# Three outer products of a kernel's first pass in the form of seven inner products instead of eight

## The chip, the cores and the metric

The kernel runs on one core of one Trainium2 chip. The metric is the device time of one execution in microseconds (us), as the median of several runs. One more execution is taken with the hardware profiler; its page and its trace are what the durations below come from. In them PE is TensorE's matmuls, PEld its weight loads, DVE is VectorE, ACT is ScalarE, POOL is GpSimd and SP is SyncE, whose queue issues nearly all DMAs.

## The reference, cut to what matters

The reference is two layers of a block, in float32, on 8 x 256 tokens of width 512. The change concerns the attention of the first layer alone:

```python
qkv = jax.nn.silu(hidden_states @ qkv_w.T)          # 2048 x 512 by 512 x 12288
...                                                 # 32 heads of 128: linear attention with decay
normed = norm_w * xf.astype(attn.dtype)             # after a root mean square over all heads
gate = jax.nn.sigmoid(hidden_states @ gate_w.T)     # 2048 x 512 by 512 x 4096
return gate * normed @ out_w.T
```

The product of tokens with the weights of q, k, v and gate is the largest piece of work in the whole computation. A mixture of 16 experts, a second attention and a low-rank layer follow or run beside it; the change doesn't touch them.

## The kernel before, in words

**Tiling.** The 2048 tokens are cut into four chunks of 512 (i = 0 to 3), the 32 heads into eight groups of four (g = 0 to 7). One unit (i, g) is the product of a chunk with the 2048 columns of weights of one group (q, k, v and gate of four heads). Four passes, one a chunk, run over the eight groups. The list `plan` (line 1071) holds all 4 x 8 x 7 outer products in their order.

**Two levels of seven.** A unit's product is a two by two block product. It is made of seven products of sums of blocks instead of eight products of blocks (Strassen's scheme in Winograd's form). These are the seven outer products, in the order `ORDER`: p1, p2, p6, p5, p3, p7, p4. Each is a two by two block product again. One inner product (`product`, line 661) is four matmuls, which work on weights of 128x512 and tokens of 128x128. In the second to fourth pass an outer product is made of seven inner products, which need weights and tokens summed a second time (inner sums). In the first pass it is made of eight, on plain blocks (`plain`, line 981).

**What the first pass makes for the others.** The weights come from the input `w_att` in four blocks of 128x512, 1 MB in all. Three outer products, p1, p2 and p4 (`RAW`, line 29), take blocks as they are. p6, p5 and p7 load one or two more operands (`block`, tag `xw`, two buffers, 1 MB each) and p3 takes p6's (`previous`), and VectorE sums them (`outer_sum`, four steps, each of one or two instructions). Then GpSimd makes four inner sums (`inner_sum`, line 634), the last of which is followed by a store of the sums to `ws`, from where the later passes load them. Plain products read the weights' four blocks, raw or with VectorE's sums, but no inner sum. Outer and inner sums are steps, kept in a list: `plain` runs those that its own outer product has left, and then, after each inner product but the first, one of the following outer product's (`following.step()`). The tokens of the first pass are in seven tiles (`first_x`), each holding four blocks; the other passes load their seven blocks from `xc`.

**Rings.** Weights are in a ring of three tiles (`big`, line 123). `prepare(n + 2)` (line 1164) makes the outer product two places on: it takes the tile of outer product n - 1 and issues its loads. The tile is free when TensorE has done n - 1's last product and the store to `ws` has landed. PSUM gives products four banks: two named `ps_a`, one `ps_b`, one `ps_e`.

**The form of seven.** In the later passes the methods `p1`, `p7`, `p6`, `p4`, `p2`, `p5`, `p3` of `Outer` (lines 1037 to 1066) issue one inner product each. Some banks are used twice: p6 adds into p1's bank, so p1's value is first copied out by ScalarE (`copied`, line 994, tag `cp`, five buffers), and likewise p7's and p6's. `p3` of an outer product runs only after `p1` and `p7` of the next. `result` (line 999) takes one of the four quarters out of its bank. Given a copy c, it adds bank and c on VectorE, and what is then still to be added is added by GpSimd (lines 1016 and 1028, by way of a buffer named r with tag `sum`, three buffers). Without a copy it adds or copies straight out of the bank, on VectorE or ScalarE.

**What runs between.** After each inner product `slot` (line 679) runs pieces that are due: the attention of a quarter (scores, attend), the output projection, and in the first pass the rows of tokens (`row`, also tag `sum`) that GpSimd scatters into `xd` for the experts.

**Order.** ScalarE's and GpSimd's instructions run in the order in which the program issues them (line 599). The orders of TensorE, VectorE and SyncE are the framework's planner's.

**The opening** (lines 140 to 523) normalizes, routes, and makes the token sums of each chunk (`token_sums`, line 369): for chunk 0 into `first_x`, for the others, with their inner sums, into `xc`.

Of the kernel before, what the change touches and what calls it, by code (L numbers as in the profile page):

```python
# [28 lines left out]
RAW = dict(p1=0, p2=1, p4=3)  # L29
# [37 lines left out]
def block_kernel(  # L67
# [25 lines left out]
    nc = tc.nc  # L93
# [73 lines left out]
    for i in range(1, NCH):  # L167
# [36 lines left out]
        out=before, in_=before, pattern=[[1, E], [-1, E]], compare_op=ALU.is_gt,  # L204
# [11 lines left out]
        out=dist[:, 0:S], in_=dist[:, 0:S], pattern=[[1, S]], compare_op=ALU.is_ge,  # L216
# [137 lines left out]
    def sub(o, a, b, eng=None):  # L354
        tt(o, a, b, ALU.subtract, eng)
# [8 lines left out]

    HC = NC // 2

    first_x, first_w = {}, []

    def token_sums(i):

        def blocks(v):
            return v.rearrange("p (c t) n -> p c t n", c=2)

        def tile_():
            return work.tile([P, 4, P], FP, tag="xsum", name="xsum", bufs=3)

        quarter = {  # L380
            (j, l): xT[i][:, bass.ts(j, HC), bass.ts(l, S)].rearrange("p c (t n) -> p c t n", t=2)
            for j, l in QUARTERS
        }
        with_ = None
        if i == 0:
            for p in ORDER:
                first_x[p] = toks.tile([P, 7, P], FP, tag="X", name="xt")
        for p, at in (
            ("p1", (0, 0)), ("p2", (1, 0)), ("p3", (1, 1)),
            ("p5", (0, 1)), ("p6", (1, 1)), ("p4", (1, 0)), ("p7", (1, 1)),  # L390
        ):
            y = quarter[at]
            if p in ("p5", "p6", "p4", "p7"):
                o = {"p5": quarter[0, 0], "p7": quarter[0, 1]}.get(p, with_)
                with_ = blocks(tile_() if i else first_x[p][:, 0:4])
                sub(with_, y, o, nc.gpsimd)
                y = with_
            if i == 0:
                if y is not with_:
                    nc.sync.dma_start(out=blocks(first_x[p][:, 0:4]), in_=y)  # L400
                continue
            nc.sync.dma_start(out=blocks(xc[i][:, ORDER.index(p), 0:4]), in_=y)
            t = tile_()
            sub(t[:, 0], y[:, 0, 1], y[:, 0, 0], nc.gpsimd)
            sub(t[:, 3], y[:, 1, 1], y[:, 0, 1], nc.gpsimd)
            sub(t[:, 1], y[:, 1, 1], t[:, 0], nc.gpsimd)
            sub(t[:, 2], y[:, 1, 0], t[:, 1], nc.gpsimd)
            nc.sync.dma_start(out=xc[i][:, ORDER.index(p), 4:8], in_=t)
# [14 lines left out]
    for i in range(NCH):  # L423
# [7 lines left out]
        if i == 0:  # L431
            for p in ORDER[0:2]:
                w = big("w")
# [21 lines left out]
        out=earlier, in_=earlier, pattern=[[1, P]], compare_op=ALU.is_gt,  # L455
# [25 lines left out]
    at = NTT * E  # L481
# [117 lines left out]
    with tc.tile_pool(name="attn", bufs=1) as attn, tc.manual_schedule(engines={mybir.EngineType.Activation, mybir.EngineType.Pool}):  # L599
# [5 lines left out]
        def weights(i, g, p, steps):  # L605

            loaded = len(first_w) > 0
            w = first_w.pop(0) if loaded else big("w")  # L610
            y = w[:, 0:4]
            v = nc.vector
            pool = nc.gpsimd

            def block(n):
                st = staged("st")[:, 0 : 16 * P].rearrange("p (b n) -> p b n", b=4)
                nc.sync.dma_start(out=st, in_=w_att[g, n])
                return st

            if i == 0:  # L620
                if not loaded:
                    nc.sync.dma_start(out=y, in_=w_att[g, dict(RAW, p6=2, p5=2, p3=1, p7=0)[p]])
                outer = dict(p6=[(add, 3), (sub, 0)], p5=[(add, 3)], p7=[(sub, 2)]).get(p, ())
                outer = [(f, block(n)) for f, n in outer]
                if p == "p3":
                    outer = [(sub, previous["s2"])]
                if p == "p6":
                    previous["s2"] = y

                def outer_sum(n):  # L630
                    for f, other in outer:
                        f(y[:, n], y[:, n], other[:, n], v)

                def inner_sum(f, o, a_, b_):
                    f(w[:, o], w[:, a_], w[:, b_], pool)
                    if o == 7:
                        nc.sync.dma_start(out=ws[g][p], in_=w[:, 4 if p in RAW else 1 : 8])

                if outer:
                    steps += [partial(outer_sum, n) for n in (1, 2, 0, 3)]  # L640
                steps += [
                    partial(inner_sum, *at) for at in ((add, 4, 0, 3), (sub, 5, 4, 1), (sub, 6, 2, 5), (sub, 7, 1, 0))
                ]
                return {at: w[:, n] for n, at in enumerate(((1, 0), (0, 0), (0, 1), (1, 1)))}
            if p in RAW:
                nc.sync.dma_start(out=y, in_=w_att[g, RAW[p]])
                nc.sync.dma_start(out=w[:, 4:8], in_=ws[g][p])
            else:
                nc.sync.dma_start(out=w[:, 1:8], in_=ws[g][p])
            return dict(zip(("p1", "p2", "p4", "p5", "p6", "p3", "p7"), (w[:, n] for n in range(1, 8))))  # L650

        def tokens(i, p):
            if i == 0:
                return {q: first_x[p][:, n] for n, q in enumerate(QUARTERS)}
            t = toks.tile([P, 7, P], FP, tag="X", name="xt")
            x_ = xc[i][:, ORDER.index(p)]
            nc.sync.dma_start(out=t[:, 0], in_=x_[:, 0])
            nc.sync.dma_start(out=t[:, 1:7], in_=x_[:, 2:8])
            return dict(zip(("p1", "p2", "p3", "p5", "p6", "p4", "p7"), (t[:, n] for n in range(7))))

        def product(bank, w, xx, first):

            for ty in range(4):
                w_ = w[:, bass.ts(ty, P)]
                a, b = (w_, xx) if ty < 3 else (xx, w_)
                mm(  # L666
                    bank[:, bass.ts(ty, P)], a, b, start=(first and ty == 0), stop=True,
                    skip_group_check=True,
                )


        pieces = []
# [6 lines left out]
        def slot():  # L679

            now[0] += 1
            n = 0
            while pieces and pieces[0][0] <= now[0] and n < (2 if len(pieces) > 12 else 1):
                f = pieces.pop(0)[2]
                f()
                n += getattr(f, "func", f).__name__ not in ("silu", "gate", "row", "scatter", "load_sum", "sums1", "sums2", "sums3", "sums4", "settle0", "settle1", "out_sum")
# [273 lines left out]
        class Outer:  # L960


            def __init__(self, unit, p):
                self.u, self.p = unit, p
                self.steps = []
                self.w = weights(unit.i, unit.g, p, self.steps)
                if unit.g == 0:
                    Outer.x_[p] = tokens(unit.i, p)
                self.x = Outer.x_[p]

            x_ = {}

            def go(self, bank, p, first=False):
                product(bank, self.w[p], self.x[p], first)
                slot()

            def step(self):
                if self.steps:
# [185 lines left out]
        def prepare(n):  # L1164
            if n < len(plan):
                outers.append(make(n))
            elif n == len(plan):
# [4 lines left out]
                for t in range(TPC):  # L1172
                    later(2 + 2 * t, lambda t=t: turn_rows(yT0, settled[0], t, ps_sc()))

        wsm = yT0 = None
        outers = [make(0), make(1)]
        for n, (i, g, p) in enumerate(plan):
            if i == 0 and p == "p5":
                for _ in range(4):
                    outers[n + 1].step()  # L1180
            cur = outers[n]
            u = cur.u
            k = ORDER.index(p)
            if k == 0:
                u.load_decay()
                if i * NG + g >= FROM:
                    for e in range(3 if i * NG + g < FROM + EARLY else 2):
                        if todo:
                            later((20 if g == 0 and i > 1 else 1) + 16 * e, partial(expert, todo.pop(0)))
                if i == 0:  # L1190
                    for e in range(2):
                        later(1 + 24 * e, partial(row, 2 * g + e))
                if i == NCH - 1 and g in (NG - 4, NG - 3):
                    low_sums(g - NG + 4)
                if (i, g) == (NCH - 1, NG - 2):
                    wrapped_up()
            if k == 2:
                u.load_decay()
            u.load_out(k)
            if i == 0:  # L1200
                prepare(n + 2)
                cur.plain(outers[n + 1])
                continue
            cur.p1()
            cur.p7()
            if plan[n - 1][0] > 0:
                outers[n - 1].p3()
            prepare(n + 2)
            cur.p6()
            cur.p4()  # L1210
            cur.p2()
            cur.p5()
# [409 lines left out]
```

## Time and profile before

| what | time |
|---|---|
| median of 3 runs | 2856.99 us (2852.0 to 2861.1) |
| the profiled execution | 2856.16 us |
| its span in the profile | 2854.4 us |
| opening (0 to 164) | 164 us |
| first pass (164 to 763) | 599 us |
| second, third and fourth pass | 607, 588 and about 574 us to the last product |
| the rest: second layer | from about 2532 us |

The page gives the busy time of each engine in the whole span, in a second part in 40 equal slices, each digit a share in tenths. Busy TensorE matmuls are pipelined, so the duration of one isn't what the next one waits: that is read from the starts. In a timeline's row stand start, length, engine, line, instruction, tile written and read, shapes, count, and in brackets how long the engine had been idle and what released it. In the table by stage, each row is a stretch with the busy time of each engine, the granted clock of TensorE, and DMA's share and rate. Line 97 is the helper `tt`, by which every add and subtract is recorded, so its rows are told apart by tiles.

### The profile page before, as it was taken

Reading aid. Unit: us, or ns where it says so; the run is one execution under the profiler, and the core shown is the slowest. Engines: PE = TensorE matmul, PEld = TensorE weight load, DVE = VectorE, ACT = ScalarE, POOL = GpSimd, SP = SyncE. Lnnn points to the kernel's source line nnn. Section 1 sums busy time; section 2 is a strip of 40 time slices with the busy share of each in tenths; the row PEclk is TensorE's granted clock in tenths of the full one; section 3 lists DMA queues with packets and bytes.
Section 4 is the critical chain, followed back from the end, with each engine's and each line's share of the span. In section 5 each row is a group of like instructions: output and inputs, shape, how many; then the busy total and the mean of one; then the engine's idle time right before and its main releaser. Section 6 shows DMA issues by size and latency. Waiting matters only on the chain. (4 is left out here: it accounts for less than half of the span.)

```text
span 2854.4 us, 49572 instructions
## 1 busy us (share of the span) xinstructions
PE 2796.7 (98%) x19864; PEld 2566.1 (90%) x19864; DVE 1569.7 (55%) x2615; ACT 948.2 (33%) x1683; POOL 1465.7 (51%) x1213
## 2 busy tenths in 40 slices
PE   8989999999999999999999999999999999999999
PEld 4469999999999999999999999999999999987877
DVE  6555666666654445444545555555555555556663
ACT  3312222212244333333443333443444333432221
POOL 4545666665546555555645454545544566552210
PEclk9999999999999999999999999999999999999999
DMA  7888998899986777778877777777777788652211
GB/s 255 301 309 337 357 352 341 341 349 347 364 320 246 262 266 273 282 270 299 296 265 257 264 266 265 259 274 280 284 259 259 267 310 298 222 212 88 76 61 61
DMA packets 161943, 763.21 MB, mean 267 GB/s; under 512 B 18209, under 2 KB 24225, under 8 KB 109874
## 3 DMA queue, kind: packets, MB, share of 16 engines
q1 hardware_dynamic: 149826, 706.25, 66.9%
q0 software_dynamic: 11888, 53.79, 5.2%
q8 instruction: 157, 2.57, 0.4%
q14 instruction: 72, 0.59, 0.1%
HBM read 596.14 MB, written 163.05 MB: 266 GB/s over the span
## 5 line engine op out<-in xcount | busy, mean ns | idle before, releaser
L666 PE MATMUL ps_a<-xt,w 128*128 128x128 f32 x5376 | 750.9, 276 | 11.7 <-DVE r L97 7.7
L666 PEld LDWEIGHTS ps_a<-xt,w 128*128 128x128 f32 x5376 | 681.9, 192 | 30.1 <-issue 14.3
L97 POOL TENSOR_TENSOR c<-c 128x512 f32<-128x512 f32 x216 | 271.7, 1273 | 262.0 <-DVE c L97 259.9
L97 POOL TENSOR_TENSOR c<-c,r 128x512 f32<-128x512 f32 x240 | 318.4, 1347 | 158.9 <-DVE r L97 153.1
L666 PE MATMUL ps_e<-xt,w 128*128 128x128 f32 x2688 | 373.4, 275 | 1.3 <-DVE c L97 1.3
L97 POOL TENSOR_TENSOR sums<-sums,sq 128x512 f32<-128x512 f32 x120 | 153.3, 1278 | 426.4 <-ACT sq L796 425.6
L996 ACT COPY cp<-ps_a 128x512 f32<-128x512 f32 x336 | 196.4, 585 | 476.0 <-PE ps_a L666 468.8
L666 PEld LDWEIGHTS ps_e<-xt,w 128*128 128x128 f32 x2688 | 344.4, 192 | 11.2 <-issue 3.8
L97 POOL TENSOR_TENSOR w<-w 128x512 f32<-128x512 f32 x224 | 294.6, 1325 | 108.2 <-issue 31.2
L666 PE MATMUL ps_a<-w,xt 128*128 128x128 f32 x1792 | 346.7, 275 | 0.0
L858 PE MATMUL ps_sc<-wo,gT 128*128 128x256 f32 x1288 | 305.1, 379 | 1.8 <-POOL gT L97 1.8
L97 DVE TENSOR_TENSOR acc<-ps_sc,acc 128x512 f32<-128x512 f32 x208 | 143.3, 690 | 265.8 <-PE ps_sc L858 198.8
L666 PEld LDWEIGHTS ps_a<-w,xt 128*128 128x128 f32 x1792 | 272.3, 192 | 0.0
L97 DVE TENSOR_TENSOR c<-ps_a,c 128x512 f32<-128x512 f32 x232 | 157.9, 686 | 202.7 <-PE ps_a L666 201.7
L858 PEld LDWEIGHTS ps_sc<-wo,gT 128*128 128x128 f32 x1288 | 232.3, 190 | 26.8 <-POOL gT L97 2.0
L666 PE MATMUL ps_b<-xt,w 128*128 128x128 f32 x1680 | 236.4, 277 | 6.8 <-ACT c L1010 4.2
L801 DVE SCALAR_TENSOR_TENSOR gT<-ps_o,nw,c 128x256 f32<-128x256 f32 x256 | 112.0, 479 | 231.0 <-ACT sq L796 222.0
L666 PEld LDWEIGHTS ps_b<-xt,w 128*128 128x128 f32 x1680 | 217.3, 194 | 17.5 <-issue 8.2
L744 ACT ACTIVATE c<-c 128x512 f32<-128x512 f32 x256 | 148.9, 627 | 170.1 <-DVE c L97 170.0
L796 ACT ACTIVATE sq<-ps_o 128x512 f32<-128x512 f32 x120 | 71.6, 597 | 382.3 <-PE ps_o L782 382.3
L666 PE MATMUL ps_e<-w,xt 128*128 128x128 f32 x896 | 173.2, 275 | 0.0
L97 DVE TENSOR_TENSOR s<-ps_sc,decay 128x384 f32<-128x384 f32 x256 | 139.8, 552 | 40.7 <-PE ps_sc L770 38.1
(299 smaller groups left out, 4635.8 us busy)
## 6 DMA issues: line engine op xcount, KB each, us to landing
w<-in_w_att_dram SPq DMA_DIRECT2D x128, 1024.0 KB
st<-in_w_att_dram SPq DMA_DIRECT2D x32, 1024.0 KB
wo<-in_w_out_dram SPq DMA_DIRECT2D x113, 256.0 KB
decay<-dec SPq DMA_DIRECT2D x64, 384.0 KB
w<-ws0p SPq DMA_DIRECT2D x12, 1792.0 KB
w<-ws1p SPq DMA_DIRECT2D x12, 1792.0 KB
w<-ws2p SPq DMA_DIRECT2D x12, 1792.0 KB
w<-ws3p SPq DMA_DIRECT2D x12, 1792.0 KB
```

Source lines behind the costliest of these rows:

```text
L97: (eng or nc.vector).tensor_tensor(o, a, b, op)
L666: mm(bank[:, bass.ts(ty, P)], a, b, start=(first and ty == 0), stop=True, skip_group_check=True,)
L744: nc.scalar.activation(qk, qk, AF.Silu)
L796: nc.scalar.activation(sq, po, AF.Square)
L801: nc.vector.scalar_tensor_tensor(gT[:, h, :].rearrange("p (t n) -> p t n", t=2), po[:, bass.ts(h, S)].rearrange("p (t n) -> p t n", t=2), ...
L858: mm(py[:, bass.ts(t, S)], self.O[p][:, hh, bass.ts(t, P)], self.wo[p][:, hh, :], start=(t == 0 and hh == 0), stop=(hh == 1), skip_group_c ...
L996: nc.scalar.copy(c, bank)
```

## The change

p1, p2 and p4 of the first pass, 24 outer products in all, are made by the methods of the form of seven; p6, p5, p3 and p7 stay in the form of eight.

- `weights` returns for these three the seven operands of the form of seven, w[:, 1] to w[:, 7], of which 4 to 7 are inner sums. The order of the four inner sums becomes 7, 4, 5, 6 (it was 4, 5, 6, 7), for all outer products, and the store to `ws` follows sum 6.
- Their token tiles get three more blocks, and one block is overwritten, by twelve GpSimd subtractions (four for each of three tiles), issued ahead of the loop over `plan`.
- The loop runs what is left of the outer product's own steps, then `p1`, `p7`, `p3` of the one before if that was in the form of seven, `prepare(n + 2)`, and `p6`, `p4`, `p2`, `p5`. `go` runs one step of the following outer product after each inner product.
- Ahead of a plain outer product, the `p3` of the one before is run, if that was in the form of seven.

```diff
+                if p in RAW:
+                    first_sums.append(t)
...
-                    if o == 7:
+                    if o == 6:
                         nc.sync.dma_start(out=ws[g][p], in_=w[:, 4 if p in RAW else 1 : 8])
...
-                    partial(inner_sum, *at) for at in ((add, 4, 0, 3), (sub, 5, 4, 1), (sub, 6, 2, 5), (sub, 7, 1, 0))
+                    partial(inner_sum, *at) for at in ((sub, 7, 1, 0), (add, 4, 0, 3), (sub, 5, 4, 1), (sub, 6, 2, 5))
                 ]
+                if p in RAW:
+                    return sums_of(w)
                 return {at: w[:, n] for n, at in enumerate(((1, 0), (0, 0), (0, 1), (1, 1)))}
...
+        def sums_of(w):
             return dict(zip(("p1", "p2", "p4", "p5", "p6", "p3", "p7"), (w[:, n] for n in range(1, 8))))

         def tokens(i, p):
+            if i == 0 and p in RAW:
+                x_ = first_x[p]
+                return dict(zip(("p1", "p7", "p2", "p3", "p5", "p6", "p4"), (x_[:, n] for n in range(7))))
...
+        for t in first_sums:
+            sub(t[:, 4], t[:, 1], t[:, 0], nc.gpsimd)
+            sub(t[:, 1], t[:, 3], t[:, 1], nc.gpsimd)
+            sub(t[:, 5], t[:, 3], t[:, 4], nc.gpsimd)
+            sub(t[:, 6], t[:, 2], t[:, 5], nc.gpsimd)
...
             def go(self, bank, p, first=False):
                 product(bank, self.w[p], self.x[p], first)
                 slot()
+                if self.following:
+                    self.following.step()
...
+        def sevenfold(n):
+
+            return plan[n][0] > 0 or plan[n][2] in RAW
...
-            if i == 0:
+            last = outers[n - 1] if n and sevenfold(n - 1) else None
+            if not sevenfold(n):
+                if last:
+                    last.p3()
                 prepare(n + 2)
                 cur.plain(outers[n + 1])
                 continue
+            if i == 0:
+                while cur.steps:
+                    cur.step()
+                cur.following = outers[n + 1]
             cur.p1()
             cur.p7()
-            if plan[n - 1][0] > 0:
-                outers[n - 1].p3()
+            if last:
+                last.p3()
             prepare(n + 2)
             cur.p6()
             cur.p4()
```

More of the change, by code (lines that the diff above doesn't have):

```diff
@@ L365, in block_kernel @@
     HC = NC // 2
-    first_x, first_w = {}, []
+    first_x, first_w, first_sums = {}, [], []
     def token_sums(i):
@@ L398, in token_sums @@
             if i == 0:
+                t = first_x[p]
                 if y is not with_:
-                    nc.sync.dma_start(out=blocks(first_x[p][:, 0:4]), in_=y)
+                    nc.sync.dma_start(out=blocks(t[:, 0:4]), in_=y)
+                if p in RAW:
+                    first_sums.append(t)
                 continue
@@ L649, in weights @@
                 nc.sync.dma_start(out=w[:, 1:8], in_=ws[g][p])
+            return sums_of(w)
+        def sums_of(w):
             return dict(zip(("p1", "p2", "p4", "p5", "p6", "p3", "p7"), (w[:, n] for n in range(1, 8))))
         def tokens(i, p):
+            if i == 0 and p in RAW:
+                x_ = first_x[p]
+                return dict(zip(("p1", "p7", "p2", "p3", "p5", "p6", "p4"), (x_[:, n] for n in range(7))))
             if i == 0:
@@ L965, in __init__ @@
                 self.steps = []
+                self.following = None
                 self.w = weights(unit.i, unit.g, p, self.steps)
```

## The prediction

> **What bounds the kernel now.** I read the page first, then busy times by stage, then the timeline of TensorE, ScalarE, SyncE, GpSimd and VectorE in the first pass, and last the waits of SyncE's queue. All times are us from the start of the span.
>
> ```profile
> PE 2796.7 (98%) x19864; PEld 2566.1 (90%) x19864; DVE 1569.7 (55%) x2615; ACT 948.2 (33%) x1683; POOL 1465.7 (51%) x1213
> ...
> DMA  7888998899986777778877777777777788652211
> ```
>
> TensorE is the bound, and in slices 3 to 11, which is the first pass, the DMA engines are 80 to 90% busy as well. By stage (columns: stretch, length, busy PE, PEld, DVE, ACT, POOL, clock, DMA share, GB/s), one group of the first pass and one of the second:
>
> ```profile
> 463.20:537.50 74.30, 74.30 (x578) 71.83 (x577) 46.72 (x73) 16.29 (x28) 47.70 (x38) 1.00 0.91 353
> ...
> 840.50:916.40 75.90, 75.90 (x580) 71.99 (x579) 33.06 (x53) 32.56 (x61) 40.48 (x33) 1.00 0.70 257
> ```
>
> A group of the first pass is 74.3 us of TensorE without a gap: what leaves TensorE there leaves the total, until something else sets the pace. DMA (0.91) and GpSimd (47.7 of 74.3) are the candidates. The second pass, already sevenfold, runs at a DMA share of 0.70. Next, what one inner product costs (TensorE's timeline):
>
> ```profile
> 612.09 0.83 PE L666 MATMUL ps_b<-xt,w 128*128 128x128 f32 x6
> 612.76 0.39 PE L666 MATMUL ps_b<-w,xt 128*128 128x128 f32 x2
> 612.98 0.83 PE L666 MATMUL ps_b<-xt,w 128*128 128x128 f32 x6
> ```
>
> The page's 275 ns of a matmul overlap. A product is eight records (four matmuls, each recorded twice: the 12,992 records of line 666 are 2 x (56 x 32 + 168 x 28)), and the next starts 0.89 later (612.09 to 612.98). So **0.89 us** is its price on the path, not 8 x 275 ns. Counting 64 weight loads to a plain outer product in the trace gives each one's start. In the group from 463 us: p1 463.2, p2 476.4, p6 489.0, p5 500.2, p3 509.4, p7 520.0, p4 527.8, next p1 537.5.
>
> [...] After one at 199.2 (weight loads):
>
> ```profile
> 201.07 1.40 PEld L666 LDWEIGHTS ps_b<-xt,w 128*128 128x128 f32 x6
> 202.35 0.55 PEld L666 LDWEIGHTS ps_b<-w,xt 128*128 128x128 f32 x2
> 202.78 1.06 PEld L666 LDWEIGHTS ps_b<-xt,w 128*128 128x128 f32 x6
> ```
>
> Here a product takes 1.71; the slow stretch costs some 1.7 us. Gaps of 1.3 and 0.8 elsewhere in the pass are followed by none. [...] the sums w<-w,st take 0.68 at the median and up to 1.77, and the long ones lie beside GpSimd's sums.
>
> **The change, part by part.**
>
> *TensorE.* p1, p2 and p4 of eight groups drop one product of eight: 24 x 0.89 = **-21.4**, all on the path.
>
> *Evacuation.* p1: four ScalarE copies stay four, three VectorE adds are new. p2 and p4: three ScalarE copies and three GpSimd adds each are new, VectorE's four stay. A group gains 6 copies (585 ns, line 996) on ScalarE, 16 busy of 74; 3 x 0.69 on VectorE, 47 busy; and 6 x 1.27 = 7.6 on GpSimd, 48 busy, in all 55 of 71.6. As busy time nothing; the cover is those engines' idle time. The order of the queues is what costs, below.
>
> *Token sums.* 12 GpSimd sums of 128x128 at 0.45 (the xsum rows when alone) = 5.4, early in the opening, where GpSimd is idle from 57.4 to 67.7, and their operands are small loads of the same opening: 0; if the gap were gone they would push the second chunk's sums by 5, which nothing waits for until the second pass.
>
> *The first two outer products.* ScalarE can't write the tiles of this stage before VectorE ends the dispatch:
>
> ```profile
> 175.33 0.58 ACT L1010 COPY c<-ps_b 128x512 f32<-128x512 f32 x1 [26.64 <-DVE disp L97]
> ```
>
> Before, p1 fills four banks (eight products, 164.4 to 171.5) and then waits. After, its third product adds into the bank whose first copy must be out, so TensorE stops after two products and has 5 of p1 plus 7 of p2 left at 176.0 where it had 8: 4 x 0.89 = 3.6 later. But TensorE then waited 1.7 at 186.7 and 2.2 at 199.2 for weights, which absorb this. So p1 and p2 of group 0 gain nothing: **+1.8**. Both bounds: 3.6 lost if the weights come later too, or another 1.7 gained if the gap at 199.2, and its slow clock, vanish.
>
> *The weights' loop.* Inner sums were off the path: plain products read only raw blocks. Now p4's second product waits for GpSimd's first inner sum, its third for the third one. The weight ring has three tiles, and p6's load of the next group needs p4's tile, which is free only after p4's last product, now behind two of the next p1. It can be followed in SyncE's, GpSimd's and VectorE's timeline:
>
> ```profile
> 612.32 0.78 SPq L622 DMA_DIRECT2D w<-in_w_att_dram  x1
> 613.15 2.06 SPq L617 DMA_DIRECT2D st<-in_w_att_dram  x2
> ...
> 633.06 0.33 SPq L617 DMA_DIRECT2D st<-in_w_att_dram  x1
> ...
> 663.33 7.78 SPq L622 DMA_DIRECT2D w<-in_w_att_dram  x2
> ```
>
> ```profile
> 599.74 5.21 POOL L97 TENSOR_TENSOR w<-w 128x512 f32<-128x512 f32 x4 [2.85 <-issue]
> ...
> 672.69 5.20 POOL L97 TENSOR_TENSOR w<-w 128x512 f32<-128x512 f32 x4 [1.82 <-PE ps_b L666]
> ```
>
> ```profile
> 638.29 3.11 DVE L97 TENSOR_TENSOR w<-w,st 128x512 f32<-128x512 f32 x2 [2.62 <-DMA st<-in_w_att_dram]
> ```
>
> p4's third sum ends at 603.7 (three of the four from 599.74). p6's load and its two blocks go out at 612.3 to 615.2, VectorE's eight sums end at 633.8, p5's block goes out at 633.1, its sums run 638.3 to 644.9, GpSimd's on p5 to 651.5, the store of p5 frees the tile that p4's load takes at 663.3, and p4's third sum ends at 676.7: a loop of 73.0. Before, it closes on nothing, since p4 didn't wait. After, from that sum to p6's load lie seven products (p6, p4, p2, p5 of p4, then p1, p7 of the next p1, then p4's p3) = 6.2, attention matmuls of 2.6 (p4 took 9.77, less 8 x 0.89) and 0.4 to the issue: 9.2 where it was 8.6. The third sums of the seven groups end at 309.5, 381.6, 455.7, 528.8, 603.7, 676.7 and 751.8, 73.7 apart on average, so 74.3 if nothing else moves; TensorE's own work is 74.3 - 3 x 0.89 = 71.6. In four of those six loops a step waits not for data but for TensorE's progress: p5's sums start 2 to 4 after the block has landed (landings 341.6, 414.9, 489.6, 562.3; starts 345.7, 419.2, 491.7, 564.8), and such steps come earlier with TensorE. Against that, GpSimd's three new adds of p2 lie beside VectorE's sums for p6 and slow two or three of these by about 1 each. I take 1.5 off the mean: a period of 72.8, so 1.2 of waiting in each of seven groups[...]: **+8.4**. Bounds: 0 (period 71.6) and 2.7 a group (74.3), further if the slow clock comes in.
>
> *Queues that loads are moved past.* In the three changed outer products, prepare comes after two or three products instead of before the first. For p6 and its two blocks the tile is the limit, counted above. p2's load waits for p7's store, p5's has 4.6 of slack at p5's start, of which it loses about 3. The inner sums' new order only brings the difference first.
>
> *Sum.* -21.4 + 1.8 + 8.4 = -11.2. The profiled execution took 2856.2 (span 2854.4 and 1.8 around it), 0.8 below the median of 2857.0; 2856.2 - 11.2 = **2845**.
>
> **Rivals.** *No wait remains*: the paced steps all move up and the slow clock at 199 goes. For it: DMA moved up to 364 GB/s in one slice, the group would need 353 x 74.3 / 71.6 = 366 on average, and early holes are left. -21.4 + 1.8 - 1.7 = -21.3: **2835**. *The loop keeps its 74.3*: for it, in the loop to 676.7 every step waits for a transfer or for sums. Seven groups give back 7 x 2.67 = 18.7: -0.9, **2855**. *Slower: the spare tiles of p4.* Its three partial results go through the three buffers named sum, one of which a token row holds until its second scatter has landed (issued at 605.1, some 7 later), and GpSimd empties them only behind p4's and the next p1's inner sums, which keep it busy from 599.7 to 611.4. The third result then waits for a buffer, VectorE is in order, and p4's last product needs that bank. If this and the weights cost 3.5 a group, it decides from 2.67 on[...]: 5.2 x 7 = 36.4, so -21.4 + 1.8 + 36.4 = +16.8: **2873**. Against it: the plan of GpSimd is ahead in the last two groups, where the weights had 3.4 of slack. That the change doesn't do what it says can't quite be: the 24 products are dropped by construction.
>
> **Chances.** Forecast 0.38, no wait 0.30, loop at 74.3 0.17, slower 0.15. About 0.3% (8.6 us) is what a measurement of this kernel can tell from no change. Faster than that: no wait, and three quarters of the forecast's spread of 2839 to 2851, 0.58; within: 0.25; slower: 0.17. The range, 2834 to 2863, holds the first three and the foot of the fourth.
>
> **What would show it.** 192 fewer records of line 666; a group of 72 to 73 us; TensorE waiting in p4 for w of GpSimd, 1 to 2 us a group; DMA share near 0.93. Wrong if the groups are 71.6 without waits (steps of the loop were paced by TensorE), or if VectorE waits for GpSimd at r and half-clock stretches follow.

## The result, and the profile after

The changed kernel takes 2887.02 us (median of 4 runs, 2882.35 to 2890.8) against 2856.9 for the kernel before in the same comparison: a ratio of 1.0105 (95% interval 1.0083 to 1.0127). Measured a second time it took 2880.06 against 2858.23, 1.0083 (1.0066 to 1.0100). It is slower by 22 to 30 us, where the forecast was 11 faster and the range ended at 2863. The profiled execution took 2887.61, with a span of 2885.9.

The page's engine line, and its DMA line by slices, of the kernel after:

```profile
PE 2800.4 (97%) x19672; PEld 2556.8 (89%) x19672; DVE 1593.2 (55%) x2639; ACT 973.6 (34%) x1731; POOL 1539.3 (53%) x1273
...
DMA  7768889988887777778777777778777778653211
```

There are 192 matmul records fewer (19864 before), so the 24 products are gone, and yet the span is 31.5 longer. Where the time went is found from the start of each outer product, counted in weight loads (64 to a plain one, 56 to one in the form of seven). In us, "again" being the second profile of the same kernel:

| kernel | opening | group 0 | groups 1 to 7 | first pass | second pass | third | fourth |
|---|---|---|---|---|---|---|---|
| before | 164.4 | 77.8 | 520.9 | 598.7 | 605.3 | 587.8 | 574.9 |
| after | 174.6 | 77.6 | 537.7 | 615.3 | 610.2 | 587.8 | 576.3 |
| after, again | 169.1 | 76.0 | 539.5 | 615.5 | 610.9 | 587.8 | 575.7 |

Nearly 17 us are lost in the first pass, in both profiles; some 5 in the second pass; the opening differs by 10.2 and by 4.7. The bounds are the starts of p1. Where the outer product ahead of a bound is in the form of seven, its last product, `p3`, comes behind the bound. So the row of after counts one product too few in group 0 and in the first pass, and one more than before in the second pass. With the bounds set after equal numbers of products, group 0 takes 79.1 against 77.8, groups 1 to 7 take 537.9 against 520.9, and the second pass 610.1 against 606.9. One by one, the groups 1 to 7 of after last 75.0, 75.7, 74.7, 75.0, 76.0, 75.8 and 85.5. The table by stage (stretch, length, busy PE, PEld, DVE, ACT, POOL, granted clock, DMA share, GB/s) of the changed kernel, groups 1 to 6 and the last:

```profile
250.00:705.00 455.00, 439.56 (x3336) 419.91 (x3335) 298.57 (x450) 119.51 (x210) 324.76 (x253) 1.00 0.89 338
705.00:790.00 85.00, 75.46 (x557) 71.32 (x555) 50.30 (x77) 19.32 (x35) 55.66 (x45) 0.98 0.87 323
```

TensorE, which had no gap in the group shown of before, is now idle for 15.4 of 455 us and for 9.5 of the last 85. DMA's share was 0.91 in that group and is lower here, so the longer groups aren't short of transfer rate. What TensorE waited for from 250 us to the end of the pass (engine, tile, line, released by: us in total, times, longest), first after, then before:

```profile
PE ps_a L677 <- DVE r L97: 13.0, 8, 5.4
PE ps_o L799 <- DVE s L97: 3.8, 6, 0.6
PE ps_a L677 <- DVE w L97: 3.4, 5, 0.9
PE ps_a L677 <- POOL w L97: 2.5, 5, 1.1
PE ps_b L677 <- DVE c L97: 2.1, 4, 0.9
```

```profile
PE ps_sc L878 <- DVE gT L801: 1.6, 3, 1.0
PE ps_o L781 <- DVE s L97: 1.3, 2, 0.6
```

The greatest is a wait for r. It is one chain, read here in one p4: VectorE's timeline, GpSimd's, and TensorE's there, one group later and at the end of the pass.

```profile
627.22 0.69 DVE L97 TENSOR_TENSOR r<-ps_e,cp 128x512 f32<-128x512 f32 x1 [5.29 <-PE ps_e L677]
628.04 0.69 DVE L97 TENSOR_TENSOR r<-ps_b,cp 128x512 f32<-128x512 f32 x1
632.75 0.69 DVE L97 TENSOR_TENSOR r<-ps_a,cp 128x512 f32<-128x512 f32 x1 [4.02 <-DMA xd<-row,slots]
```

```profile
626.50 1.00 POOL L1115 DMA_INDIRECT xd<-row,slots  x1 [0.16 <-issue]
627.52 5.21 POOL L97 TENSOR_TENSOR w<-w 128x512 f32<-128x512 f32 x4
632.68 2.50 POOL L97 TENSOR_TENSOR c<-c,r 128x512 f32<-128x512 f32 x2
```

```profile
633.50 0.94 PE L677 MATMUL ps_a<-xt,w 128*128 128x128 f32 x6 [1.50 <-DVE r L97]
...
710.07 0.94 PE L677 MATMUL ps_a<-xt,w 128*128 128x128 f32 x6 [2.23 <-DVE r L97]
...
789.98 2.05 PE L677 MATMUL ps_a<-xt,w 128*128 128x128 f32 x8 [5.43 <-DVE r L97]
```

Two of the three buffers hold the first two results from 627 on; GpSimd adds these only at 632.7, behind four inner sums of the next outer product. The third buffer holds a token row, whose scatter is issued at 626.50 and lets VectorE go on at 632.75, 6.25 later. VectorE stood for 4.02 with the third result at its head, and TensorE's last product of p4 stood behind it. The same wait costs 5.43 at the end of the pass; the longer record there (eight records in 2.05, where six take 0.94 above) runs at a granted clock of 0.50.

Half clock stands behind two of these three gaps. Behind the 5.43 the granted clock is 0.50 from 789.9 to 793.3, behind the 2.23 from 711.4 to 714.8; behind the 1.50 it stays at 1.00. In the trace that the prediction read, it is 0.50 from 200.0 to 203.4, behind the gap of 2.24 before 199.26.

### The profile page after: what moved, and what is told of

The parts are those of the page before. It is cut to its first block, busy times and chain, and to the rows that moved or that the text cites. A ratio compares the mean times of both kernels' runs of the same rounds, so it can differ in the third digit from the quotient of the medians.

```text
span 2885.9 us, 49418 instructions
## 1 busy us (share of the span) xinstructions
PE 2800.4 (97%) x19672; PEld 2556.8 (89%) x19672; DVE 1593.2 (55%) x2639; ACT 973.6 (34%) x1731; POOL 1539.3 (53%) x1273
## 5 line engine op out<-in xcount | busy, mean ns | idle before, releaser
L97 POOL TENSOR_TENSOR c<-c 128x512 f32<-128x512 f32 x240 | 303.0, 1276 | 296.3 <-DVE c L97 293.9
L97 POOL TENSOR_TENSOR c<-c,r 128x512 f32<-128x512 f32 x264 | 347.9, 1338 | 158.9 <-DVE r L97 156.4
L1017 ACT COPY cp<-ps_a 128x512 f32<-128x512 f32 x384 | 224.2, 584 | 607.3 <-PE ps_a L677 572.9
L97 DVE TENSOR_TENSOR c<-ps_a,c 128x512 f32<-128x512 f32 x216 | 146.6, 686 | 197.7 <-PE ps_a L677 196.1
L677 PE MATMUL ps_b<-xt,w 128*128 128x128 f32 x1536 | 216.0, 277 | 5.6 <-DVE mv L232 2.6
L677 PEld LDWEIGHTS ps_b<-xt,w 128*128 128x128 f32 x1536 | 199.0, 193 | 17.5 <-issue 9.7
L814 ACT ACTIVATE sq<-ps_o 128x512 f32<-128x512 f32 x120 | 71.6, 597 | 335.2 <-PE ps_o L800 335.2
```

What stands on the lines that cost most here:

```text
L97: (eng or nc.vector).tensor_tensor(o, a, b, op)
L677: mm(bank[:, bass.ts(ty, P)], a, b, start=(first and ty == 0), stop=True, skip_group_check=True,)
L814: nc.scalar.activation(sq, po, AF.Square)
L1017: nc.scalar.copy(c, bank)
```

## The experiments

**Theory:** the row's buffer makes p4's third result late; that is most of the loss in the first pass. **Rival:** the weights' loop of the prediction holds the groups at 74.3 or above anyway. For the opening: the twelve token sums are in its way, or its half-clock stretches fall otherwise by chance. Measured, with the first pass of each profile split at the starts of p1 as above (e6, e9 and e10 compute other values and serve for their times alone):

| run | us | ratio to before (95% interval) | opening | group 0 | groups 1 to 7 |
|---|---|---|---|---|---|
| e1_tokens_only | 2859.33 | 1.0006 (0.9993 to 1.0020) | 166.6 | 77.6 | 520.2 |
| e2_row_own_buffer | 2864.54 | 1.0005 (0.9993 to 1.0017) | 168.4 | 77.7 | 521.1 |
| e3_p1_p2_only | 2865.39 | 1.0021 (1.0010 to 1.0031) | 168.1 | 80.9 | 522.4 |
| e4_p4_only | 2880.52 | 1.0087 (1.0060 to 1.0114) | 162.1 | 79.4 | 542.4 |
| e5_split_store | 2869.68 | 1.0025 (1.0008 to 1.0042) | 176.6 | 77.2 | 526.8 |
| e6_no_p5_store | 2895.2 | 1.0123 (1.0084 to 1.0162) | 176.8 | 73.9 | 549.2 |
| e7_p5_sums_early | 2874.52 | 1.0058 (1.0034 to 1.0081) | 162.0 | 79.4 | 531.4 |
| e8_split_and_early | 2864.64 | 1.0018 (1.0007 to 1.0030) | 174.1 | 78.8 | 521.3 |
| e9_drop_24 | 2846.7 | 0.9969 (0.9956 to 0.9981) | 168.2 | 76.9 | 508.3 |
| e10_raw_operands | 2858.04 | 0.9999 (0.9986 to 1.0011) | 165.1 | 73.1 | 518.0 |
| e11_p1_p2_row | 2864.26 | 1.0024 (1.0013 to 1.0036) | 169.9 | 81.4 | 522.9 |
| e12_after_again | 2880.06 | 1.0083 (1.0066 to 1.0100) | 169.1 | 76.0 | 539.5 |

The time of the kernel before in these comparisons was 2858.2 to 2859.6.

**The token sums alone**, put into the kernel before, their results unused:

```diff
+        for t in first_sums:
+            sub(t[:, 4], t[:, 1], t[:, 0], nc.gpsimd)
+            sub(t[:, 6], t[:, 3], t[:, 1], nc.gpsimd)
+            sub(t[:, 5], t[:, 3], t[:, 4], nc.gpsimd)
+            sub(t[:, 6], t[:, 2], t[:, 5], nc.gpsimd)
```

> The kernel before, with the twelve token sums of the first chunk added on GpSimd and read by nobody (the overwriting one goes to a spare block); the outer products stay in the form of eight. Theory A: these sums are what made the opening 10.2 us longer (164.4 to 174.6 us), through the order of the opening's work; then the opening takes about 174 and the whole about 2867. Theory B: the opening was longer because TensorE ran at half clock in it for 41 us instead of 20, and where that falls hangs on small shifts, not on the sums; then the opening lies anywhere from 164 to 174, and the groups of the first pass stay at 74.3 us.

No difference in the whole (1.0006), 2.2 us in the opening. They cost nothing that can be measured, as the prediction had it; the opening's 10.2 need another reason.

**The row in a buffer of its own**, nothing else:

```diff
-x_ = attn.tile([P, C], FP, tag="sum", name="row", bufs=3)
+x_ = attn.tile([P, C], FP, tag="sq", name="row", bufs=1)
```

> The changed kernel, with the token rows of the first pass in the buffer sq, which this pass does not use, so that p4's three partial results have the three buffers named sum to themselves. Theory A (VectorE waits for a row's scatter before it can write p4's third partial result, and TensorE for that): the waits of 1 to 2.4 us a group before p4's last product and 5.7 us at the end go, with the slow clock behind the last two; groups 73.5 to 74 instead of 75.4, the last group about 75 instead of 85.5, in all about 20 us less than the changed kernel, 2867. Theory B (the weights' loop sets the pace): the wait turns up again at p4's or p6's weights, groups stay at 75, only the last group gains, 2877.

TensorE's waits in the first pass of this kernel, to be set beside those of after:

```profile
PE ps_o L799 <- DVE s L97: 3.8, 6, 0.6
PE ps_a L677 <- DVE w L97: 3.4, 5, 0.9
PE ps_a L677 <- POOL w L97: 2.9, 4, 1.2
PE ps_b L677 <- DVE c L97: 2.1, 4, 0.9
```

The line of r is gone, the other four are nearly as they were, and the groups 1 to 7 take 16.6 less, 10.3 of it in the last. The theory holds. The 16.6 are for the most part the waits of 13.0; the half clock from 711.4 to 714.8 adds some 1.7 by estimate (half of 3.4). But what is left is the kernel before's 520.9 again, not some 19 less. That is the figure which the rival named; whether the loop is its cause, e5 to e10 try.

**Which outer products.** Only p1 and p2, then only p4, in the form of seven:

```diff
+SEV = ("p1", "p2")          # or ("p4",), in place of RAW in the four new tests
```

> The changed kernel with p1 and p2 alone in the form of seven, p4 in the form of eight (eight token sums instead of twelve). Theory A (p4's partial results are the cost): no wait for a buffer is left, groups 74.3 - 1.8 + about 0.9 of waiting for p6's weights = 73.4, total 2857 - 7 plus what the opening has lost, 2850 to 2860. Theory B (the later release of weight tiles is the cost): p6's load is as early as before, since p4 is plain, so p6 doesn't wait, but p5's load is later; groups 72.5 to 74.3.

> The changed kernel with p4 alone in the form of seven (four token sums). Theory A (p4's partial results wait for a row's scatter): groups 74.3 - 0.9 + 1.6 = 75.0, the last one and the step into the second pass about 10 longer, total 2857 + 5 + 8 = 2870, less if the opening is as before. Theory B (cost is in p6 behind p2, not in p4): groups 73.4, total about 2850.

p4 alone loses more in the groups than the three together: its groups 1 to 6 take 75.6 to 80.5. Its greatest wait (p4 only, the pass from 250 us):

```profile
PE ps_a L678 <- DVE r L98: 15.5, 6, 3.9
```

That is 15.5 in six waits. Behind one of 1.86, ended at 394.4, two lots of six records take 1.49 each, which took 0.83 at a clock of 1.00 in before. p1 and p2 alone save 16 products and still gain nothing (ratio 1.0021, groups of 73.4 to 75.9), which neither of the two theories for e3 had.

**The loop of weights**, on top of the row's own buffer: the store of p6, p5, p3 and p7 in two parts, the first without inner sums (e5); no store of p5 at all, the later passes loading p6's sums in its place (e6); p5's outer sums ahead of p6's products (e7); e5 and e7 together (e8).

```diff
+                    if o == 7 and p not in RAW:                     # e5
+                        nc.sync.dma_start(out=ws[g][p][:, 0:3], in_=w[:, 1:4])
...
-                    if o == 6:
+                    if o == 6 and p != "p5":                        # e6
...
+                for _ in range(4 if self.p == "p6" else 0):         # e7, in plain
+                    following.step()
```

> As the run before with the rows in their own buffer, and the store of p6, p5, p3 and p7 split: blocks 1 to 3 (VectorE's sums) go out ahead of the first inner sum, the four inner sums after the last. Theory A (the weights' loop sets the pace of 74.1 to 74.7 us a group: p5's store has to land before p4's load goes out): the last part is 1 MB instead of 1.75, lands some 4 us earlier, groups 71.8 to 72.8, total 10 to 15 us under the run with the rows alone. Theory B (what is left comes from the order of VectorE and GpSimd around p6, not from the loop): groups stay at 74.

> As the run with the rows in their own buffer, with the store of p5's sums left out (the later passes load p6's in their place, so that these passes compute with other weights in the same time). Theory A (loop): p4's load goes out when TensorE has done with p5, some 9 us earlier, no wait is left before p4's third product, groups 71.6 plus the wait of 0.9 before attend, 72.0 to 72.6, total about 2850. Theory B: groups stay at 74.

> As the run with the rows in their own buffer, with p5's four outer sums put ahead of p6's first product instead of behind its second to fifth (VectorE began them 5 us after their block had landed). Theory A (loop, with a link that VectorE's order makes late): p5's sums start 3 to 5 us earlier, p4's weights with them, groups 72 to 73. Theory B: VectorE waits for the block with four of p6's banks behind it, TensorE waits for banks, groups 74 to 75.

> Rows in their own buffer, split store and early p5 sums together: the version in which the loop is shortest with the output unchanged. Theory A: the loop is 7 to 9 us shorter, TensorE's own work and the wait before attend are left, groups 71.8 to 72.5, total about 2848, under the kernel before. Theory B: groups 73 to 74, total as the kernel before.

Three misses for the loop: neither the store in two parts nor the earlier sums shorten the groups, nor do both (526.8, 531.4, 521.3 for seven groups, against e2's 521.1). Without p5's store the groups 1 and 2 take 72.7 and 72.9, where e2 has 74.2 and 74.7. That speaks for the loop, but from group 4 on each loses some 7 us to another wait. VectorE's and TensorE's timeline of e6 there:

```profile
482.48 0.69 DVE L97 TENSOR_TENSOR acc<-ps_sc,acc 128x512 f32<-128x512 f32 x1 [0.97 <-PE ps_sc L896]
491.63 0.69 DVE L97 TENSOR_TENSOR w<-w,st 128x512 f32<-128x512 f32 x1 [8.46 <-DMA w<-in_w_att_dram]
492.24 0.68 DVE L97 TENSOR_TENSOR c<-ps_b,cp 128x512 f32<-128x512 f32 x1
492.84 0.68 DVE L97 TENSOR_TENSOR w<-w,st 128x512 f32<-128x512 f32 x1
493.44 0.68 DVE L97 TENSOR_TENSOR c<-ps_a,cp 128x512 f32<-128x512 f32 x1
```

```profile
494.18 1.65 PE L677 MATMUL ps_a<-xt,w 128*128 128x128 f32 x6 [6.86 <-DVE c L97]
```

It is the same trap as p4's, at p2: a sum that needs a load stands ahead of the emptying of two banks in VectorE's order, the sum starts 9.6 us after the load's issue at 482.01, and TensorE waits for the banks. So e6 doesn't settle the loop; the next two take its terms apart.

**Taking the terms apart.** The kernel before with one product of p1, p2 and p4 left out (e9); after, with the row's buffer, with raw blocks for the inner sums as operands (e10).

```diff
+                        if self.p not in RAW or n < 3 or k == 0:    # e9, in plain
                             product(bank, self.w[i, k], self.x[k, j], k == 0)
...
-                    return sums_of(w)                               # e10, RAW in the first pass
+                    return dict(zip(("p1", "p2", "p4", "p5", "p6", "p3", "p7"), (w[:, n] for n in (1, 2, 3, 0, 1, 2, 3))))
```

> The kernel before, with the last inner product of p1, p2 and p4 of the first pass simply left out (one of the two terms of one quarter is missing); no operand, order, wait or buffer is otherwise changed. It isolates the term of -21.4 us. Theory A (the 2.67 us a group are there to be had, and only the new waits of the form of seven eat them): groups of the first pass at 71.6 to 72.0, the time 18 to 21 below the kernel before. Theory B (the group's transfers and weight sums need some 74 us by themselves, before, too, they were close behind TensorE): groups stay at 73.5 to 74.3 with TensorE waiting for w of VectorE, the time within 7 of the kernel before.

> The kernel after with the rows' own buffer, and with the products of p1, p2 and p4 taking raw blocks of the weights in place of inner sums (the values are other ones); the inner sums are still made and stored, all copies, adds and banks of the form of seven stay. No product of the first pass then waits for an inner sum, so the weights' loop doesn't close on GpSimd. If the loop holds the groups (theory A): 71.6 to 72.5 us, some 14 to 18 us less in the first pass than the 598.8 measured with the rows' own buffer alone. If the banks' evacuation through the in-order VectorE holds them (theory B), or the transfers: 73.5 to 74.7, as there.

e9 is faster by 0.31%, and its groups 2 to 7 take 72.1 to 73.3: neither the 71.6 of its first theory nor the 74 of its second. Its waits in the pass, and then those of e10:

```profile
PE ps_o L781 <- DVE s L97: 3.8, 6, 0.6
PE ps_sc L878 <- DVE gT L801: 2.5, 2, 1.4
```

```profile
PE ps_a L677 <- DVE w L97: 3.5, 5, 0.9
PE ps_o L799 <- DVE s L97: 3.1, 5, 0.6
PE ps_b L677 <- DVE c L97: 2.5, 4, 1.2
```

e9 needs no evacuation of the new kind (emptying of banks by way of copies) and no inner sum: 12.6 less in groups 1 to 7 is what fewer products are worth here. With no inner sum as operand the groups of e10 still take 73.2 to 75.2, nearer to its second theory. Of the two causes which that theory names, the transfers by themselves can't be it: e9 moves the same weights in groups of 72.1 to 73.3. A wait for w lies at p6's first product, 0.88 at 558.63. VectorE's timeline ahead of it:

```profile
552.38 0.69 DVE L97 TENSOR_TENSOR c<-ps_e,cp 128x512 f32<-128x512 f32 x1 [0.27 <-PE ps_e L677]
552.99 0.55 DVE L97 TENSOR_TENSOR s<-ps_sc,decay 128x384 f32<-128x384 f32 x1
553.46 3.33 DVE L97 TENSOR_TENSOR w<-w,st 128x512 f32<-128x512 f32 x4
556.71 0.68 DVE L97 TENSOR_TENSOR acc<-ps_sc,acc 128x512 f32<-128x512 f32 x1
557.30 0.68 DVE L97 TENSOR_TENSOR c<-ps_b,cp 128x512 f32<-128x512 f32 x1
557.90 2.48 DVE L97 TENSOR_TENSOR w<-w,st 128x512 f32<-128x512 f32 x4
```

VectorE has no gap from 552.38 on: p6's eight sums and the emptying of p2's banks (c with cp) fall into the same eight us, and the sum that p6 needs first comes out too late. This is read from the one place; no run moves the sums or the emptying apart.

**p1 and p2 with the row's buffer** (e3 and e2 together), and **the kernel after once more**:

> p1 and p2 alone in the form of seven, p4 in the form of eight, rows in a buffer of their own: 16 products less. p4's last product no longer waits for an inner sum or a spare buffer. Theory A (p4 closes the loop): groups at 72.5 to 73.0, the first pass 586 to 590, and if the opening's clock falls as before, 8 to 12 below the kernel before. Theory B (p6's outer sums and transfers set some 74): 74 to 75, no gain, 0 to +6.

> The kernel after once more, unchanged, to see how much of the 10.2 us in the opening belongs to it. If the half-clock stretches of the opening fall by chance from run to run: a mean clock between 0.986 and 0.991 over the runs, times from 2875 to 2890. If they belong to the program: 0.986 to 0.988 in each run, 2882 to 2891 as before.

e11 is as e3 (522.9 and 522.4) and within its second theory: the row's buffer matters to p4 alone, and taking p4 out brings no gain. e12 repeats the first pass within 1 us, with an opening 5.5 shorter; its runs show a clock of 0.988 to 0.991, those of the first comparison 0.986 to 0.988. So the opening's length isn't fixed by the program.

## Why the prediction was wrong

The step that failed by most is how p4's results leave the banks. The prediction's sum puts nothing for p4's third result waiting for a spare buffer. It has this as a rival with a chance of 0.15 and sets it aside, because GpSimd's plan is ahead in the last two groups. The runs show 16.6 us for it in groups 1 to 7, and 10.3 of them in the last group. Three more terms were wrong: TensorE's -21.4 was too large, evacuation wasn't free, and the opening, put at 0, took 10.2 and 4.7 longer.

The steps for groups 1 to 7, from one kernel to the next (before, e9, e10, e2, after):

| step | us |
|---|---|
| 21 products fewer (e9 less before, 508.3 - 520.9) | -12.6 |
| copies, sums, banks and order of the form of seven (e10 less e9, 518.0 - 508.3) | +9.7 |
| waits for inner sums (e2 less e10, 521.1 - 518.0) | +3.1 |
| the row in p4's ring (after less e2, 537.7 - 521.1) | +16.6 |
| sum | +16.8 |

Each entry is one profile less another, and after and its second profile differ by 1.8, so some two us of an entry are noise. Two entries also hold moved work: the groups 1 to 7 contain 878 matmul records of attention and output projection in before, 886 in e9 and 898 in e10, e2 and after; group 0 and the second pass have that many fewer. At some 0.2 us each, by the starts of such records, that is an estimate of about 1.5 in the first entry and 2.7 in the second.

- **TensorE, -21.4.** The records are right, the size isn't. 21 x 0.89 = 18.7 in these groups shrank to 12.6 even with nothing added. TensorE's idle time rose from 2.9 to 6.9 (520.9 less 518.0 busy, 508.3 less 501.4), and most of the rest is the moved work. Attention's second product now waits 0.6 for VectorE's s in nearly every group. That wait was right behind the path: the list of before has it twice, but the group that the prediction showed has no gap, and so nothing of how close the next limit was. "71.6" was a bound and not a period.
- **Evacuation, 0.** Wrong: 9.7 less the moved work is about 7, so 1.0 a group, with VectorE 66% and ScalarE 26% busy in groups 1 to 6 of after (298.57 and 119.51 of 455). As busy time it costs nothing, but it comes in a burst, at the very place where VectorE makes p6's sums; and a bank that was free after one evacuation is now waited for (w 0.9, c up to 1.2). The entry holds whatever else the new order moves; that the burst is all of it isn't shown.
- **The weights' loop, +8.4.** Inner sums cost 0.4 a group and not 1.2. With the rows out of the way (e2) the groups stand at 74.1 to 75.2, where the rival "the loop keeps its 74.3" put them, but by another route: e10, in which no product waits for an inner sum, stays within 3.1 of e2, so most of the 18.7 was gone before inner sums came in.
- **Group 0, +1.8.** Its mechanism shows: TensorE's gap before the first copies grows from 4.20 (ended at 176.0) to 7.76 (ended at 186.2), the 3.6 of the prediction, and the next gap falls from 1.68 to 0.87. Its size doesn't: with equal products the group takes 1.3 longer, where -2.7 and +1.8 would make it 0.9 shorter, and 18 records of moved work left it besides. With raw operands it takes 4.6 less than in e2, so here the waits for inner sums, with the half clock behind them, are most of the rest (in after one of 1.41, ended at 247.0, with a clock of 0.50 from 247.2 to 250.6).
- **The rival "the spare tiles of p4"**, given 0.15, is what happened: buffer, scatter, GpSimd's queue and VectorE's order, step by step as it was written. Its price of 5.2 a group, 36.4 in all with the weights, was the author's estimate, with a slow stretch in every group, and too high: 16.6 and 3.1 in seven groups, and half clock stands behind two of the eight waits for r. That its total of +16.8 is also the sum of the table is chance, since the terms differ. The reason against it, that GpSimd's plan is ahead in the last two groups, was wrong where it mattered. GpSimd's scatter and VectorE's third result in the last group:

```profile
781.08 1.00 POOL L1115 DMA_INDIRECT xd<-row,slots  x1 [0.15 <-issue]
...
789.15 0.69 DVE L97 TENSOR_TENSOR r<-ps_a,cp 128x512 f32<-128x512 f32 x1 [5.84 <-DMA xd<-row,slots]
```

  GpSimd had emptied the other two buffers by 785.1; only the scatter held the third result.
- **The second pass, 0.** It takes some 5 longer in both profiles; with equal products, 3.2 and 3.8. TensorE waits there for an expert's rows, and a granted clock of 0.50 from 882.1 to 885.5 follows:

```profile
881.08 0.66 PE L724 MATMUL ps_sc<-ident,xw 128*128 128x128 f32 x4 [2.24 <-DMA xw<-xd]
```

  The load is issued at 870.50, ten us ahead. In e12, e2 and e4 the same wait is 2.3 to 2.5. It stands in eight of the nine profiles with p4 in the form of seven (not in e6) and in none of the five without (before, e1, e3, e9, e11). So it goes with p4's form; that the shifted order of the loads causes it is argued, not shown.
- **The opening, 0.** 10.2 and 4.7 longer in the two profiles. The token sums don't do it (e1). Its code is the kernel before's in e9, and still it took 168.2. Between 100 and 120 us stand, in this order, before, e9, after and after again:

```profile
100.00:120.00 20.00, 19.24 (x67) 9.38 (x67) 15.11 (x31) 6.17 (x13) 13.24 (x17) 1.00 0.72 272
```

```profile
100.00:120.00 20.00, 19.24 (x59) 8.77 (x59) 16.73 (x31) 5.46 (x11) 14.29 (x17) 0.83 0.68 255
```

```profile
100.00:120.00 20.00, 19.24 (x43) 7.15 (x41) 14.41 (x26) 3.48 (x9) 14.65 (x18) 0.66 0.66 249
```

```profile
100.00:120.00 20.00, 19.24 (x51) 7.81 (x50) 14.43 (x26) 3.46 (x7) 15.84 (x21) 0.68 0.63 236
```

  The granted clock is 1.00, 0.83, 0.66 and 0.68. Over the whole opening the half-clock stretches add up to 20.5, 27.3, 41.0 and 34.1 us. If half of every us at half clock is lost, the last three should be 3.4, 10.2 and 6.8 longer than before by this estimate; they measure 3.8, 10.2 and 4.7. So the clock accounts for the opening to within some 2 us. Part of it falls otherwise without any change of code; whether the changed kernel makes it likelier stays open.

The total, with equal products: 10.2 in the opening, 1.3 in group 0, 17.0 in groups 1 to 7, 3.2 in the second pass and -0.2 after it give 31.5, the difference of the two spans. No version that computes the whole beat the kernel before. e9 shows that leaving these 24 products out of the kernel before, with nothing added, is worth about 11 us.

## What to carry to other kernels

A product taken out of a gapless engine is worth its full price only down to the next wait (here 12.6 of 18.7), and a gapless trace doesn't show how near that is: leave the product out and look (e9) before building what replaces it. Where VectorE empties results out of banks, what decided here wasn't its busy share but what stood at its head: in after a result waiting for a buffer shared with a row (4.02 and 5.84 idle, the scatter issued 6.25 and 8.07 before VectorE goes on), in e6 a sum waiting for a load (8.46 idle). Give tiles with a transfer's lifetime a ring of their own (one line, 16.6 us).

## What the runs showed of the hardware that was not expected

The same kernel's time varied with the granted clock: over 20 runs, e2 took 2854.7 us at 0.992 and 2871.0 at 0.988. Half-clock stretches stood in the opening at 100 us in some profiles and not in others (before and e9, granted clock 1.00 and 0.83 from 100 to 120), with the same code there and TensorE busy for 19.24 of 20 us in both.

The length of a gap alone didn't tell here whether half clock follows. In after a gap of 1.41, ended at 247.0, is followed by a clock of 0.50 from 247.2 to 250.6, and the longer one of 1.50, ended at 633.5, by 1.00. In before the gap of 1.7 at 186.7 is followed by 1.00 too. In e10 two gaps of 1.91 and 1.92, ended at 770.9 and 849.2, have slow products behind them: six records take 1.26 and 1.39, where they take 0.83 ahead of the gaps. What else decides it was not shown.
